# First attention of a graph-network stack on Trainium2: key projection ahead of its bank's copies, tile ends a step later, first logits amid diffusion, last two row tiles as plain products

## The chip, the cores and the metric

The kernel runs on one core of one Trainium2 chip. Its five engines are TensorE (PE, with the weight loads shown apart as PEld), VectorE (DVE), ScalarE (ACT), GpSimd (POOL) and SyncE (SP, which here issues the DMAs). The metric is the device time of one execution in microseconds; the median of several runs counts.

## The reference

A stack of four graph layers works on 3327 nodes with 256 features and a dense weighted adjacency `adj` (3327 x 3327). Each layer's output is added to its input and normalised. The change lies in layer 3, which runs two rounds of "top-p attention" and diffusion:

```python
q = X @ W1.T @ W2.T
k = X @ W3.T
probs = softmax(q @ k.T)                       # (N, N)
# per row: keep the largest probabilities until 0.9 of the mass is reached
A = probs * mask;  A = A / A.sum(-1)
...
for n in range(2):
    A = top_p_attention(Xa, W1, W2, W3)
    Xf = R @ Xf                                # R = (adj + I) / row sums: diffusion
    Xa = A @ Xa                                # attention
    Z = Z + Xf @ U1[n].T + Xa @ U2[n].T
out = layernorm(X + Z)
```

All arithmetic is in 32-bit floats.

## The kernel before, in words

The rows are cut into nt = 26 tiles of 128, and these into nh = 13 pairs (tiles 2i and 2i+1). `X` holds the features of all tiles in SBUF. The code of layers 0 to 2 and of the second round of layer 3 is the same in both kernels.

**Two products in the first round.** The first round computes, for each pair, the diffusion of its two row tiles (`diffused_pair`) and their attention (`attended_pair`). Both treat the pair as a 2 x 2 block product and do it in Strassen's manner with seven products of 128 columns each (`products`, PE) instead of eight; `b` holds the precombined blocks of `X` (in `G`'s memory), `cb` and `sw` are DVE's combinations of the other operand, and `assembled` (DVE) puts the sums in `acc` together into `c`. A diffusion pair has 13 steps; every second step issues three DMAs for an `at` buffer (three of them) and one DVE operation for `cb` (one part ahead). Tile 0's diffusion is done in layer 2's end, and tile 1's by `diffused_first`, which is a plain product of 26 blocks, 256 columns wide. An attention pair has 13 steps too; each transposes four 128 x 128 blocks of `e` with PE (`turn`) into a PSUM bank named `tp`, of which there are two, copies them to `wt` with ACT, and mixes them into `sw` with DVE three steps ahead.

**The kept rows.** `logits(t)` starts tile t: `scores` multiplies the queries with all keys in four chunks, through the one PSUM buffer `sc`, and ACT copies each chunk into `e`. POOL writes the padding columns of `e` (`L1137`). `search_short` then finds the cut: DVE takes the 8 largest of each of 26 segments (`cand`), ranks the candidates in six rounds (`top`, `rest`), ACT takes the exponential of the row (`L1382`), and DVE masks `e` in two halves. `look()` runs one step of the search at the head of the queue.

**A tile's ends.** `first` finishes a row tile in four steps: ACT scales the attention's row sums (`L1532`, into `c` itself); PE transposes the diffused row `xf` and the scaled one, and DVE copies them to `xt`; PE multiplies with `U1` and `U2` (six products), DVE adds `X` into `s`, which is sent to `sd`; PE multiplies with the second `U2` into the bank `pg`, ACT copies it to `g` (a buffer named `s`, `L1558`), which is sent to `gd`, and `key_and_query` multiplies with `wkq` into the same bank, from which ACT takes the key (`L901`) and the query (`L903`), and SP sends the query to `qd`.

**The order.** In the first round PE and DVE keep the program's order (`Fixed`, with `fixed = True`); ACT, POOL and SP are ordered by a scheduler. Most instructions of the round therefore have the helper's line, L891, and are told apart by their tiles. For each pair i the loop runs a first `stage` of seven steps (a diffusion step of pair i+1 each; the score chunks of tile 2i+2 on even steps, the ends of tile 2i-2 on odd ones; at step 5 `attend_to` finishes the search of tile 2i+1 and transposes the first blocks), then seven attention steps, then a second `stage` of six steps (scores of tile 2i+3, ends of tile 2i-1), and the other six attention steps. After the last pair the ends of tiles 24 and 25 follow one after the other.

Of the kernel before, what the change touches and what calls it, by code (L numbers as in the profile page):

```python
# [18 lines left out]
P = 128  # L19
# [31 lines left out]
def gnn_kernel(ctx: ExitStack, tc: tile.TileContext, n: int, a: dict, out: bass.AP):  # L51
# [816 lines left out]
    with tc.tile_pool(name="l3", bufs=1) as pool, tc.tile_pool(name="l3d", bufs=1, space=DRAM) as dram:  # L868
# [23 lines left out]

        tensor, vector = Fixed(nc.tensor), Fixed(nc.vector)

        def key_and_query(work, ps, p, it, xt):

            h, j = divmod(it * P, half)
            for k in range(2):
                tensor.matmul(ps, wkq[h][:, k, :], xt[:, k, :], start=(k == 0), stop=(k == 1))
            key, query = (slice(x * DA, (x + 1) * DA) for x in (h, 1 - h))  # L900
            nc.scalar.copy(kT[p][key, j:j + P], ps[key, :])  # L901
            q = work.tile([2 * DA, P], F32, name="q")
            nc.scalar.copy(q[query, :], ps[query, :])  # L903
            for x in (0, DA):
                nc.sync.dma_start(qd[p][it, x:x + DA, :], q[query, :])

        xf0 = F[:, nt - 1, :D]
        q0 = F[:, nt - 2, :P]
# [396 lines left out]
            nc.vector.scalar_tensor_tensor(d, acc, rd, t, op0=ALU.mult, op1=ALU.add)  # L1305
            out.append(d)

        def attended(work, psum, e, rhs, tp=2, copy=nc.scalar.copy):

            acc = psum.tile([P, D], F32, name="acc")  # L1310
            for j0 in range(0, nt, 4):
                m = min(4, nt - j0)
                pt = psum.tile([P, 4, P], F32, name="tp", bufs=tp)
                for j in range(m):
                    nc.tensor.transpose(pt[:, j, :], e[:, (j0 + j) * P:(j0 + j + 1) * P], ident)
                wt = work.tile([P, 4, P], F32, name="wt", bufs=3)
                copy(wt[:, :m, :], pt[:, :m, :])
                for j in range(m):
                    nc.tensor.matmul(acc, wt[:, j, :], rhs[:, j0 + j, :],  # L1319
                                     start=(j0 + j == 0), stop=(j0 + j == nt - 1))  # L1320
                yield None
            yield acc
# [199 lines left out]
        def normalizer(sm, kept, total):  # L1522

            f = t1(sm, "f")
            vector.scalar_tensor_tensor(f, total, 1e-12, kept, op0=ALU.mult, op1=ALU.max)
            vector.reciprocal(f, f)
            return f

        def first(work, psum, it, acc, f, xf, tag="pj"):

            xa = acc if tag == "tp" else work.tile([P, D], F32, name="h")
            nc.scalar.mul(xa, acc, f)  # L1532
            yield
            pt = psum.tile([P, 4, P], F32, name=tag)
            for i, v in enumerate((xf, xa)):
                for k in range(2):
                    tensor.transpose(pt[:, 2 * i + k, :], v[:, k * P:(k + 1) * P], ident)
            xt = work.tile([P, 4, P], F32, name="xt", bufs=1)
            vector.tensor_copy(xt, pt)
            yield  # L1540
            ps = psum.tile([P, 4, P], F32, name=tag).rearrange("p (k x) d -> p k (x d)", k=2)
            for k in range(4):
                tensor.matmul(ps[:, 0, :], xt[:, k, :], (u1 if k < 2 else u2)[:, 0, k % 2, :], start=(k == 0), stop=(k == 3))
            for k in range(2):
                tensor.matmul(ps[:, 1, :], xt[:, k, :], u1[:, 1, k, :], start=(k == 0), stop=(k == 1))
            s = work.tile([P, D], F32, name="s")
            vector.tensor_add(s, ps[:, 0, :], X[:, it, :])
            nc.sync.dma_start(sd[it], s)
            nc.scalar.copy(Y[:, it, :], ps[:, 1, :])
            yield  # L1550
            pg = psum.tile([P, 4, P], F32, name=tag).rearrange("p (k x) d -> p k (x d)", k=2)
            for k in range(2):
                tensor.matmul(pg[:, 0, :], xt[:, 2 + k, :], u2[:, 1, k, :], start=(k == 0), stop=(k == 1))
            if tag == "pj":
                nc.scalar.copy(G[:, it, :], pg[:, 0, :])
            else:
                g = work.tile([P, D], F32, name="s")
                nc.scalar.copy(g, pg[:, 0, :])  # L1558
                nc.sync.dma_start(gd[it], g)
            key_and_query(work, pg[:, 1, :P], 1, it, xt[:, 2:, :])  # L1560
            yield

        def second(work, psum, it, acc, f, xf):
# [48 lines left out]
        def both(*parts):  # L1612

            parts = list(parts)
            while parts:
                parts = [x for x in parts if next(x, parts) is not parts]

        with tc.tile_pool(name="l3w", bufs=2) as work, tc.tile_pool(name="l3s", bufs=4) as sm:
# [13 lines left out]
            with tc.tile_pool(name="l3p", bufs=2, space=PSUM) as psum, tc.tile_pool(name="l3a", bufs=1) as quads:  # L1632
                fixed = True
                es, searches, xfs, todo, queue = {}, {}, [xf0], [], []
                flat = G.rearrange("p t d -> p (t d)")
                b = blocks(X, [flat[:, k * nh * HD:(k + 1) * nh * HD].rearrange("p (t d) -> p t d", t=nh) for k in range(4)])

                def look():
                    while queue and next(queue[0], queue) is queue:
                        queue.pop(0)  # L1640

                def finish():
                    while queue:
                        look()

                def logits(t):
                    return start(0, t, es, searches, search_short) if t < nt else iter(())

                def spreading(i):
                    x = diffused_pair(quads, psum, i, b, xfs) if i < nh else iter(())  # L1650
                    next(x, None)
                    return x

                def stage(spread, steps, groups, ends, then=lambda: None):
                    for k in range(steps):
                        next(spread, None)
                        if k % 2:
                            next(ends, None)
                        else:
                            next(groups, None)  # L1660
                        if k == 5:
                            then()
                        look()
                    for _ in groups:
                        pass
                    for _ in ends:
                        pass

                def attend_to(i):
                    turned[0] = attended_pair(quads, psum, (es[2 * i], es[2 * i + 1]), b)  # L1670
                    finish()
                    next(turned[0])

                turned = [None]
                for _ in logits(0):
                    pass
                queue.append(searches[0])
                for _ in diffused_first(quads, psum, 1, xfs):
                    look()
                spread = spreading(1)  # L1680
                for _ in logits(1):
                    look()
                finish()
                queue.append(searches[1])
                for _ in range(8):
                    look()
                for i in range(nh):
                    ends = todo or [iter(()), iter(())]
                    stage(spread, 7, logits(2 * i + 2), ends[0], lambda: attend_to(i))
                    values = turned[0]  # L1690
                    if i + 1 < nh:
                        queue.append(searches[2 * i + 2])
                    for _ in range(7):
                        next(values)
                        look()
                    stage(spread, 6, logits(2 * i + 3), ends[1])
                    for _ in spread:
                        pass
                    finish()
                    if i + 1 < nh:  # L1700
                        queue.append(searches[2 * i + 3])
                    for k in range(6):
                        if k == 3:
                            spread = spreading(i + 2)
                        next(values)
                        look()
                        if k % 3 == 2:
                            look()
                    c = next(values)
                    todo = []  # L1710
                    for r in range(2):
                        it = 2 * i + r
                        f = normalizer(sm, kepts[0][:, it:it + 1], tots[0][:, it:it + 1])
                        todo.append(first(quads, psum, it, c[:, r, :], f, xfs[it], "tp"))
                        next(todo[r])
                for x in todo:
                    both(x)
                fl0 = unresolved(sm, psum, 0)
                fixed = False
            for x in (slice(0, JH), slice(JH, nt)):  # L1720
# [209 lines left out]
```

## Time and profile before

| what | value |
|---|---|
| median of 3 runs | 3494.32 us (3488.72 to 3496.67) |
| the profiled execution | 3488.59 us; its span 3486.7 us; mean granted PE clock 0.965 |
| busy share of the span | PE 90%, PEld 74%, DVE 79%, ACT 50%, POOL 27% |
| first attention's first scores / second attention's first scores (PE) | 1696.3 us / 2624.1 us |
| one pair of the middle | 68.46 us (the same instruction at 2059.89 and 2539.10, seven pairs apart) |

The shares are means over the whole span. For a change inside one stage the tables of waits and the timeline of that stage say more: a line of the timeline has the start, the duration, the engine, the tile written and the tiles read, the count of merged instructions, and in brackets the engine's idle time before it and what ended it. A time in the table of waits belongs to the engine that stood still; the engine after the arrow is the one whose result came last.

### The profile page before, as it was taken

To read this page: it belongs to the slowest core of one execution; us is meant where nothing else is said; L and a number is where in the kernel's file an instruction comes from. 1 tells how busy PE (TensorE), PEld (TensorE's weight loads), DVE (VectorE), ACT (ScalarE), POOL (GpSimd) and SP (SyncE) were. 2 spreads that over 40 slices of the span, in tenths; PEclk is the share of its full clock that TensorE was granted. 3 is DMA by queue.
4 is the path that set the end of the run, shared out by engine and by line. 5 is a ranking of instruction groups with operands and counts; after the bars stand their busy time and mean duration, and the time that the engine had idled before them with its cause. 6 is when DMAs were issued, how large, how long until landed. Compare 5 with 4: busy or idle time off the path is not lost. (4 is left out here: it accounts for less than half of the span.)

```text
span 3486.7 us, 50559 instructions
## 1 busy us (share of the span) xinstructions
PE 3154.8 (90%) x18379; PEld 2568.2 (74%) x18379; DVE 2759.1 (79%) x6406; ACT 1742.3 (50%) x2763; POOL 939.7 (27%) x942
## 2 busy tenths in 40 slices
PE   8999888888987777999899999999978999999996
PEld 5998767666665555888688888888865777777775
DVE  4665368999999997777577777787755999999996
ACT  1000556767767773111233333333326888888883
POOL 0000245666666652111400000000002333333332
PEclk9999999999999988999899999999998999999998
DMA  5775334334333222444222222222213122222220
GB/s 196 256 250 180 116 95 124 109 105 120 109 105 87 68 56 99 152 143 149 94 71 71 79 76 69 82 69 84 63 34 108 56 63 71 62 66 69 63 66 16
DMA packets 206264, 344.31 MB, mean 99 GB/s; under 512 B 22222, under 2 KB 129166, under 8 KB 205870
## 3 DMA queue, kind: packets, MB, share of 16 engines
q1 hardware_dynamic: 205998, 340.92, 32.1%
q8 instruction: 148, 2.42, 0.3%
q14 instruction: 118, 0.97, 0.1%
HBM read 304.65 MB, written 36.21 MB: 98 GB/s over the span
## 5 line engine op out<-in xcount | busy, mean ns | idle before, releaser
L330 POOL TENSOR_TENSOR h<-du,row 128x2048 f32<-128x2048 f32 (+1 forms) x110 | 465.8, 4235 | 344.3 <-DVE hc L330 247.2
L330 DVE TENSOR_TENSOR_SCAN h<-dA,carry,h 128x512 f32<-128x512 f32 (+1 forms) x384 | 449.1, 1221 | 18.5 <-ACT dA L337 18.4
L337 ACT ACTIVATE dA<-t,A_log 128x512 f32<-128x512 f32 (+1 forms) x448 | 293.3, 660 | 147.8 <-DVE h L330 146.3
L1286 PE MATMUL acc<-F,at 128*128 128x256 f32 x1352 | 352.1, 386 | 0.0
L1319 PE MATMUL acc<-G,wt 128*128 128x256 f32 x1352 | 335.0, 391 | 6.0 <-ACT wt L1130 5.5
L1070 PE MATMUL acc<-F,at 128*128 128x257 f32 x1352 | 302.1, 380 | 0.9 <-ACT r L1014 0.9
L389 PE MATMUL cb<-F,at 128*128 128x256 f32 x1196 | 295.0, 395 | 8.2 <-ACT hn L409 3.4
L1319 PEld LDWEIGHTS acc<-G,wt 128*128 128x128 f32 x1352 | 249.1, 192 | 65.2 <-ACT wt L1130 35.6
L1286 PEld LDWEIGHTS acc<-F,at 128*128 128x128 f32 x1352 | 238.5, 190 | 72.2 <-issue 47.8
L680 PE MATMUL y<-ident,hc 128*128 128x128 f32 x1664 | 238.5, 298 | 46.8 <-DVE hc L330 46.5
L1070 PEld LDWEIGHTS acc<-F,at 128*128 128x128 f32 x1352 | 252.4, 190 | 36.2 <-issue 1.1
L680 PEld LDWEIGHTS y<-ident,hc 128*128 128x128 f32 x1664 | 212.4, 155 | 87.0 <-DVE hc L330 62.8
L389 PEld LDWEIGHTS cb<-F,at 128*128 128x128 f32 x1196 | 229.7, 198 | 58.3 <-issue 19.9
L1137 POOL MEMSET e<- 128x1 f32 x52 | 4.9, 99 | 930.8 <-PE tp L891 807.1
L330 DVE TENSOR_TENSOR hc<-h,row 128x2048 f32<-128x2048 f32 (+2 forms) x114 | 243.8, 2140 | 11.3 <-PE y L680 4.3
L891 PEld LDWEIGHTS acc<-X,at 128*128 128x128 f32 x988 | 143.5, 194 | 49.0 <-issue 44.8
L891 PE MATMUL acc<-X,at 128*128 128x128 f32 (+1 forms) x988 | 177.9, 292 | 0.0
L891 PE MATMUL acc<-G,sw 128*128 128x128 f32 x1014 | 169.7, 276 | 6.0 <-DVE sw L891 6.0
L138 PE MATMUL acc<-t,cb 128*128 128x128 f32 (+1 forms) x1014 | 168.4, 275 | 0.0
L1253 ACT COPY wt<-tp 128x512 f32<-128x512 f32 x169 | 98.7, 588 | 131.8 <-PE tp L891 117.0
L891 PEld LDWEIGHTS acc<-G,sw 128*128 128x128 f32 x1014 | 140.3, 192 | 8.2 <-DVE sw L891 8.1
L891 DVE MAX8 cand<-e 128x8 f32<-128x128 f32 x676 | 140.8, 278 | 0.0
(412 smaller groups left out, 7095.1 us busy)
## 6 DMA issues: line engine op xcount, KB each, us to landing
at<-in_adjT SPq DMA_DIRECT2D x54, 832.0 KB, 4.4
at<-in_adjT SPq DMA_DIRECT2D x130, 320.0 KB, 3.0
row<-bc SPq DMA_DIRECT2D x80, 512.0 KB, 5.0
at<-in_adjT SPq DMA_DIRECT2D x52, 640.0 KB, 5.3
at<-in_adjT SPq DMA_DIRECT2D x52, 576.0 KB, 3.8
at<-in_adjT SPq DMA_DIRECT2D x72, 256.0 KB, 3.1
at<-mixed SPq DMA_DIRECT2D x72, 256.0 KB, 3.6
mixed<-cb SPq DMA_DIRECT2D x26, 640.0 KB, 3.9
```

What stands on the lines that cost most here:

```text
L138: mm = nc.tensor.matmul(acc, w[:, j, :], x, start=(y == 0 and k % 3 == 0 and k < 6), stop=(y == nh - 1 and k in (2, 6)))
L330: return lambda *x, **k: tc.keep_in_program_order(op(*x, **k))
L337: decays.append(op(*x, **k))
L389: ten.matmul(acc, at[:, j % JC, :], X0[:, j, :], start=(j == 0), stop=(j == nt - 1))
L680: x = ten.matmul(y[:, g * P:(g + 1) * P], h[:, g, i * P:(i + 1) * P], ident, is_transpose=True, start=(first and g == 0), stop=(last and g ...
L891: return lambda *x, **k: tc.keep_in_program_order(op(*x, **k))
L1070: nc.tensor.matmul(acc, at[:, j, :], F[:, j0 + j, :], start=(j0 + j == 0), stop=(j0 + j == nt - 1))
L1137: nc.gpsimd.memset(e[:, n:], NEG)
L1253: nc.scalar.copy(wts[-1], pt)
L1286: nc.tensor.matmul(acc, at[:, j, :], rhs[:, j0 + j, :], start=(j0 + j == 0), stop=(j0 + j == nt - 1))
L1319: nc.tensor.matmul(acc, wt[:, j, :], rhs[:, j0 + j, :], start=(j0 + j == 0), stop=(j0 + j == nt - 1))
```

## The change

There are five edits, all in the first round.

1. `key_and_query` is split. In `first`, the product with `wkq` now stands right behind the product with `U2` into the same bank, ahead of ACT's copy to `g`; the copies of key and query follow that copy.
2. In `stage`, the ends run at steps 2, 3 and 4 instead of 1, 3 and 5.
3. The score chunks of tile 1 are put between the four groups of `diffused_first`, with three `look()` after each group, where they followed it with one; pair 1's first `at` part is requested ahead of it. Seven instead of eight `look()` follow.
4. The loop over pairs runs to nh - 1, that is to pair 11. Tiles 24 and 25 are then done one by one by `attended`: 26 blocks, each a transposition and one product of 256 columns with `X`, in seven groups of four, the transpositions one group ahead and with four `wt` buffers. The ends of tiles 22 and 23, and then of 24, run between the groups; two `look()` per group of tile 24 finish the search of tile 25.
5. `first` takes the tile that it scales into as an argument.

```diff
+        def project_keys(ps, it, xt):
+            h = it * P // half
             for k in range(2):
                 tensor.matmul(ps, wkq[h][:, k, :], xt[:, k, :], start=(k == 0), stop=(k == 1))
+        def store_keys(work, ps, p, it):
...
-        def attended(work, psum, e, rhs, tp=2, copy=nc.scalar.copy):
+        def attended(work, psum, e, rhs, tp=2, copy=nc.scalar.copy, acc=None):
...
+            def turn(j0):
                 m = min(4, nt - j0)
                 pt = psum.tile([P, 4, P], F32, name="tp", bufs=tp)
                 for j in range(m):
+                    tensor.transpose(pt[:, j, :], e[:, (j0 + j) * P:(j0 + j + 1) * P], ident)
+                wts.append(work.tile([P, 4, P], F32, name="wt", bufs=4 if fixed else 3))
+                copy(wts[-1][:, :m, :], pt[:, :m, :])
+            if fixed:
+                turn(0)
+                yield None
+            for j0 in range(0, nt, 4):
+                if not fixed:
+                    turn(j0)
+                elif j0 + 4 < nt:
+                    turn(j0 + 4)
+                wt = wts.pop(0)
+                for j in range(min(4, nt - j0)):
+                    tensor.matmul(acc, wt[:, j, :], rhs[:, j0 + j, :],
...
-            key_and_query(work, pg[:, 1, :P], 1, it, xt[:, 2:, :])
+            project_keys(pg[:, 1, :P], it, xt[:, 2:, :])
+            g = G[:, it, :] if tag == "pj" else work.tile([P, D], F32, name="s")
+            nc.scalar.copy(g, pg[:, 0, :])
+            if tag != "pj":
                 nc.sync.dma_start(gd[it], g)
+            store_keys(work, pg[:, 1, :P], 1, it)
...
                     for k in range(steps):
                         next(spread, None)
-                        if k % 2:
+                        if k % 2 == 0:
+                            next(groups, None)
+                        if k in (2, 3, 4):
                             next(ends, None)
-                        else:
-                            next(groups, None)
...
+                spread = spreading(1)
+                groups = logits(1)
                 for _ in diffused_first(quads, psum, 1, xfs):
-                    look()
-                spread = spreading(1)
-                for _ in logits(1):
-                    look()
+                    next(groups, None)
+                    for _ in range(3):
+                        look()
+                for _ in groups:
+                    pass
                 finish()
                 queue.append(searches[1])
-                for _ in range(8):
+                for _ in range(7):
                     look()
-                for i in range(nh):
+                for i in range(nh - 1):
...
-                for x in todo:
-                    both(x)
+                values = attended(quads, psum, es[nt - 2], X, acc=psum.tile([P, 2, 512], F32, name="acc")[:, 0, :D])
+                next(values)
+                ends = (x for y in todo for x in y)
+                for it in (nt - 2, nt - 1):
+                    for _ in range(7):
+                        acc = next(values)
+                        if it == nt - 2:
+                            look()
+                            look()
+                        next(ends, None)
+                    acc = next(values)
+                    if it == nt - 2:
+                        finish()
+                        values = attended(quads, psum, es[nt - 1], X, acc=psum.tile([P, 2, 512], F32, name="acc")[:, 0, :D])
+                        next(values)
+                    f = normalizer(sm, kepts[0][:, it:it + 1], tots[0][:, it:it + 1])
...
+                    for _ in ends:
+                        pass
+                    ends = first(quads, psum, it, acc, f, xfs[it], "tp", c)
+                    next(ends)
+                both(ends)
```

## The prediction

> **What bounds the kernel now.** I read the table by stage first: the first attention of layer 3 runs from 1706 to 2624 us, and its middle repeats every 68.46 us (one pair of row tiles). The waits of the tensor engine in it, longest first (columns: total us, times, longest), name what the diff is about:
>
> ```profile
> PE tp L891 <- ACT c L1532: 24.5, 13, 5.6
> PE tp L891 <- ACT s L1558: 17.3, 26, 1.9
> PE acc L891 <- DVE sw L891: 8.1, 24, 1.3
> ...
> PE acc L891 <- DVE cb L891: 3.7, 1, 3.7
> ```
>
> PE stands for the scaled rows `c` and for the copy into `s`. Counted on the weight loads, so with the drained pipeline, one pair loses 1.67 us to `c` and 2 x 0.86 us to `s`. But what PE waits for is only worth its length if nothing else is as late. So next the table by windows for one pair (columns: window, length, then busy us of PE, PEld, DVE, ACT, POOL):
>
> ```profile
> 2057.96:2083.44 25.48, 22.94 (x179) 19.71 (x177) 23.02 (x84) 9.35 (x15) 0.20 (x2) 1.00 0.26 75
> 2083.44:2100.90 17.46, 16.80 (x121) 14.17 (x120) 11.70 (x33) 5.90 (x13) 0.00 (x0) 1.00 0.34 100
> 2100.90:2126.42 25.52, 25.52 (x203) 23.05 (x202) 17.15 (x60) 9.16 (x12) 0.00 (x0) 1.00 0.19 56
> ```
>
> The first window begins at the last diffusion product of a pair (I call it L) and ends at the first product with `U1` of the next (U). Its DVE share is the highest of the three, and the timeline of DVE there has one idle interval over a tenth of a us, at its start, then none until 2082.35:
>
> ```profile
> 2058.27 0.29 DVE L891 COPY c<-acc 128x128 f32<-128x128 f32 x1 [0.31 <-PE acc L891]
> ...
> 2078.66 0.69 DVE L891 TENSOR_TENSOR cb<-at 128x512 f32<-128x512 f32 x1
> ...
> 2079.05 0.44 PE L891 MATMUL tp<-ident,c 128*128 128x128 f32 x2 [1.44 <-ACT c L1532]
> ...
> 2079.78 0.39 PE L891 MATMUL acc<-G,cb 128*128 128x128 f32 x2
> ...
> 2080.03 0.68 DVE L891 COPY xt<-tp 128x512 f32<-128x512 f32 x1
> ...
> 2083.55 2.75 PE L891 MATMUL tp<-U,xt 128*128 128x256 f32 x12
> ```
>
> So from L to U the vector queue decides: it starts on the sums of L and runs through. From U to the next L, PE decides. That the wait for `c` ends at 2079.05 and the `cb` of the very next diffusion step at 2079.35 is the line to remember. Third, the tail: from 2551.51 to 2624.12 PE works 50.97 of 72.61 us, with a hole of 5.65 us and a cold clock:
>
> ```profile
> 2557.65 0.69 PE L891 MATMUL tp<-ident,c 128*128 128x128 f32 x2 [5.65 <-ACT c L1532]
> ...
> 2559.12 3.36 PE L891 MATMUL tp<-U,xt 128*128 128x256 f32 x7 [0.78 <-DVE xt L891]
> ...
> 2569.33 0.76 PE L891 MATMUL tp<-ident,e 128*128 128x128 f32 x5 [1.42 <-DVE e L891]
> ```
>
> **What the Trainium skill says.** "PSUM — Partial Sum Buffer", section on bank collisions: two engines may not touch one bank in the same quadrants at once, and the software must order them. This is the 0.86 us: `wkq`'s product goes into the bank from which ACT is copying `s`; the trace agrees. "TensorE: Matmul & The Clock Gate", section "Architectural detail": ACT and DVE queues are strictly first in, first out. The trace agrees: `cb` at 2078.66 starts as `f` ends. Same page, "What's actually happening": after an idle window of about 3.4 us the array runs at half rate until it has been busy as long. Here 8 weight loads of the `U` product take 3.06 us at 2559.12, against 12 in 2.46 us at 2083.44.
>
> **The unit prices**, from the timeline at full clock: a diffusion step 1.56 us (2073.01 to 2074.57), a score chunk 0.90, four transposes 0.44, an attention step with them 2.00, a 256-wide instruction 0.22 (two a product). One tile's ends: 0.44 (transposes), 2.68 (six `U` products), 0.90 + 0.45 (`pg`, `wkq`), 4.5 together.
>
> **Part 1, the loop (11 pairs have ends).** Removed: the waits for `s` (2 x 0.86) and for `c` (1.67), 3.4 us a pair if nothing came in their place. I follow the two queues instead.
>
> L to U: DVE runs the same list up to the `cb` of step k=0, ending 21.4 us after L (2079.35 - 2057.96). PE now does step k=2 before the transposes, and the third product of that step needs this `cb`. PE gets there about 2077.4 and waits 1.9 us: the wait for `c` becomes one for `cb`. Then 1.12 (rest of the step) + 0.90 + 0.44 + 1.56 (k=3) = 4.02, so U stands 25.46 after L, against 25.48: nothing gained. The copy `xt` now sits behind two rank rounds (0.82 each) and the second `cb`; it ends about 24.9 after L, 0.5 before it is needed.
>
> U to L: the first tile's `pg` and `wkq` lose 0.86 of wait; PE reaches the transposes of `e` 8.16 after U instead of 8.85 (2092.29 - 2083.44). The second masked half of `e` is ready at 8.44, and only the fourth transpose needs it, at 8.5: 0 to 0.25 us of new wait, I take 0.1. The 0.44 for `q` gives way to about as long for the third bank's `wt`: 0 to -0.1. The second tile's `pg` and `wkq` (1.35 us) stood after L, under DVE's list, and now stand before L, because ends come at k=4 and the last diffusion step at k=5: +1.35 on the path. Its 0.86 of wait stood after L too and was hidden, so nothing comes back for it. Sum: -0.69 + 0.1 - 0.05 + 1.35 - 0.02 = **+0.7 us a pair, +7.5 in all**. Both ends: -2 a pair, if DVE makes up the time (its slack of 0.3 at L says it doesn't), +2 if `xt` is late as well.
>
> The DMAs of the ends move with them. `sd` needs `s` after U, and lands about 1.8 us later (2564.67 to 2566.45); `g` may be written 3.8 us after U's end, so it stays hidden, with SP's three loads of `at` (1.7 us) between.
>
> **Part 2, the tail.** The loop ends one pair sooner, and tiles 24 and 25 are plain. PE's work goes up: 26 x 2 x 0.22 + 26 x 0.11 = 14.4 us a tile, 28.8 against 13 x 2.00 = 26.0. But tile 24 needs no kept rows of tile 25, so its products fill the hole while DVE masks tile 25, and the ends of 22 to 24 stand between groups. From 2551.5 on: 28.8 + 4 x 4.5 = 46.8 of work; waits: `c` of tile 22 about 2.8 (one group covers 2.7 of the hole), the first `wt` of tile 25 behind `q` and `c` on ACT 1.0, banks 1.2, cold clock 2.0; last chain: scaling 0.8, `xt` 1.2, and `s`, its DMA, `g`, `kT`, `q` past the last product 2.3. Sum 58.1, against 72.6: **-14.5**, ends -8 and -20. Earlier `wkq` spares 0.7 us of this at the very end (ACT copies follow each other where PE stood between). After it the order on all five queues is as before, so nothing else moves. Passing the scaled tile as an argument issues no instruction.
>
> **Part 3, the head.** Scores of tile 1 go between groups of `diffused_first`; before, PE took from 1719.7 to 1732.3 for them. But ACT has the exponential of tile 0 ahead of their first copy, and that needs the last segment of tile 0, whose padding POOL writes at 1714.75, after 23 scalings `F`. So copy 1 ends near 1720, PE stops after the second group, and diffusion pairs start near 1729, 3.3 us sooner. DVE's `F` of tile 1 now waits for the last group (about 1728), then the halves (3.9), 26 maxima (5.1) and two rounds: `cb` at 1740.3 instead of 1741.8. **-1.5**, ends -5 and +1. Loading pair 1 ahead puts 640 KB and three issues (1.8 us of SP) before the groups' loads; PE starts at 1706.4, so it costs 0 to 1.
>
> **Sum:** +7.5 - 14.5 - 1.5 = -8.5 us on the profiled 3488.6 us, so 3480. That execution is the fastest of those shown, 5.7 under the median of 3494.3, so against the median about **3485**. A measurement of this kernel can tell about 0.2% (7 us).
>
> **Rivals.** *The waits simply go* (PE is the bound throughout): 11 x 3.4 = 37, tail 17, head 3: -57, 3437. PE's 90% and the waits table speak for it, DVE's unbroken run from L to U against it. *Loop and tail cancel*: a tail of -10 and a loop of +8: 3491. *Slower, by DVE's chain*: `xt` behind `cb` and two rounds misses its 0.5 us of slack. If it is late by 1.8, U slips 1.3, and with 0.7 the pair costs 2 us: 22 - 10 (tail at its short end) - 1.5 = +10.5, 3505. It decides from 1.7 us a pair on at that tail, 2.1 at mine. The gap-free DVE list speaks for it; that the rounds ahead of `xt` are the same ones that already ran, against it.
>
> **Chances:** my forecast 0.52, the waits go 0.12, cancel 0.26, slower 0.10. So faster 0.64, same 0.26, slower 0.10. The forecast alone spans 3475 to 3493; the range goes on to 3460, for a part of the waits going, and to 3498.
>
> **What would show it.** Right: no PE wait for `c` in the loop but one of about 1.9 us for `cb` a pair; DVE's wait for `acc` at `c` up from 0.3 to about 1.6; a period near 69.2 us; second attention's first scores 58 us after the last paired product. Wrong: a period under 67, or PE idle from 2551.5's place to the second attention for more than 16 us.

## The result, and the profile after

The change made the kernel a little faster: 3479.06 us median (3474.8 to 3481.12) against 3494.32, ratio 0.9956 with a 95% interval of 0.9941 to 0.9971. The forecast said 3485, 3460 to 3498, with faster as the likeliest case. Measured anew at the end of the study, the ratio was 0.9973 (0.9961 to 0.9985), or 9.4 us less (5 to 14) at a kernel before of some 3490 us; the profiled executions differ by 9.5 us (3488.59 and 3479.06). The two intervals overlap (10 to 21 us and 5 to 14), and the traces speak for the lower one: the first attention, from its first scores to those of the second, is 9.7 us shorter in one trace of the changed kernel and 9.0 in the other. So the change is worth about 9 to 10 us.

The waits of PE in the first attention, after (columns as before: total us, times, longest):

```profile
PE acc L891 <- DVE cb L891: 23.6, 12, 6.2
PE acc L891 <- DVE sw L891: 18.5, 36, 1.3
...
PE tp L891 <- ACT wt L1262: 2.9, 12, 0.2
PE tp L891 <- ACT c L1553: 2.5, 1, 2.5
PE sc L1154 <- ACT q L907: 1.9, 1, 1.9
```

Read against the same table of before: 24.5 us of waits for `c` shrank to one, in the tail; the 17.3 us for `s` are gone. In their place stand 23.6 us for `cb` (3.7 before) and 18.5 for `sw` (8.1 before). Head and tail are in these sums: 6.2 of the 23.6 is one wait in the head, where the 3.7 stood. In the loop alone (1750 to 2550 us), 15.8 us for `c` and 10.2 for `s` went, and 17.4 for `cb` and 9.5 more for `sw` came: there the waits changed their names and kept their length. One pair by windows after (length, then busy us of PE, PEld, DVE, ACT, POOL; granted clock, DMA share, GB/s), cut at L, at U and between, as before:

```profile
2063.09:2088.66 25.57, 22.19 (x171) 18.89 (x169) 23.18 (x84) 8.48 (x12) 0.20 (x2) 1.00 0.22 65
2088.66:2106.15 17.49, 17.25 (x129) 15.16 (x128) 12.29 (x35) 5.96 (x14) 0.00 (x0) 1.00 0.33 99
2106.15:2132.12 25.97, 25.97 (x204) 23.40 (x202) 16.44 (x58) 9.73 (x15) 0.00 (x0) 1.00 0.23 66
```

From L to U it still takes 25.5 us, with PE busy less of it (22.19 us for 22.94) and DVE as much as before (23.18 for 23.02): PE waits for a list that is as long as it was. From U to the next L, the two other windows, it is 43.46 us for 42.98, and there PE has hardly an idle moment. The timeline of DVE and PE there, with the waits in brackets:

```profile
2063.39 0.29 DVE L891 COPY c<-acc 128x128 f32<-128x128 f32 x1 [1.63 <-PE acc L891]
...
2076.48 0.49 PE L891 MATMUL acc<-G,sw 128*128 128x128 f32 x2 [1.26 <-DVE sw L891]
...
2083.75 0.69 DVE L891 TENSOR_TENSOR cb<-at 128x512 f32<-128x512 f32 x1
2084.50 0.49 PE L891 MATMUL acc<-G,cb 128*128 128x128 f32 x2 [1.54 <-DVE cb L891]
...
2087.41 0.69 DVE L891 COPY xt<-tp 128x512 f32<-128x512 f32 x1 [0.72 <-PE tp L891]
2088.77 2.75 PE L891 MATMUL tp<-U,xt 128*128 128x256 f32 x12
```

DVE now waits 1.63 us for the sums of L, where it waited 0.31: L itself is late. Then it runs 20.4 us without a stop to `cb` at 2083.75, PE stands for that `cb`, and `xt` is ready 0.7 us ahead of U. That is the picture the forecast had drawn. The tail after:

```profile
2562.14 1.99 PE L891 MATMUL acc<-X,wt 128*128 128x256 f32 x8 [0.28 <-ACT wt L1328]
...
2566.85 0.69 PE L891 MATMUL tp<-ident,c 128*128 128x128 f32 x2 [2.49 <-ACT c L1553]
...
2609.31 3.72 PE L891 MATMUL tp<-U,xt 128*128 128x256 f32 x16 [0.78 <-DVE xt L891]
...
2615.55 0.97 PE L1154 MATMUL sc<-kT,q 64*128 64x416 f32 x4 [1.93 <-ACT q L907]
```

The hole of 5.65 us in front of `c` is 2.49 us. The last paired product, that of pair 11, ends at 2560.8, and the second attention's first scores stand 54.7 us behind it. In the kernel before, in which one more pair follows, they stand 72.6 us behind the same product.

### The profile page after: what moved, and what is told of

Same layout as the page of the kernel before. It is cut to its first block, busy times and chain, and to the rows that moved or that the text cites. A ratio compares the mean times of both kernels' runs of the same rounds, so it can differ in the third digit from the quotient of the medians.

```text
span 3477.3 us, 50356 instructions
## 1 busy us (share of the span) xinstructions
PE 3155.6 (91%) x18301; PEld 2570.0 (74%) x18301; DVE 2743.7 (79%) x6359; ACT 1738.5 (50%) x2764; POOL 938.9 (27%) x942
## 5 line engine op out<-in xcount | busy, mean ns | idle before, releaser
L891 PE MATMUL acc<-G,sw 128*128 128x128 f32 x936 | 157.2, 277 | 14.5 <-DVE sw L891 14.5
L1262 ACT COPY wt<-tp 128x512 f32<-128x512 f32 x156 | 90.4, 587 | 132.8 <-PE tp L891 116.6
L891 PE MATMUL acc<-G,cb 128*128 128x128 f32 x624 | 122.6, 278 | 23.6 <-DVE cb L891 23.6
L1403 ACT ACTIVATE e<-e,neg 128x3328 f32<-128x3328 f32 x26 | 79.8, 3070 | 127.6 <-DVE neg L891 119.6
```

Source lines behind the costliest of these rows:

```text
L891: return lambda *x, **k: tc.keep_in_program_order(op(*x, **k))
```

## The experiments

All runs are compared with the kernel before on the same chip; "us" below is the ratio times 3490. To see where a pair's time lies I cut it, in every trace, at the start of DVE's first copy of L's sums (called L here), at the six `U` products of the first tile (U), and at those of the second (U2). The pairs from the third on agree within 0.15 us, those of cb_twice apart; "both of these" is mask_early_keys_late:

| kernel | L to U | U to U2 | U2 to L | pair | ratio (95% interval) | us |
|---|---|---|---|---|---|---|
| before | 25.28 | 36.24 | 7.01 | 68.53 | | |
| keys_only | 25.28 | 35.77 | 7.01 | 68.06 | 0.9964 (0.9951-0.9978) | -12.6 |
| ends_only | 25.39 | 36.06 | 9.05 | 70.50 | 1.0077 (1.0059-1.0094) | +26.9 |
| tail_only | 25.27 | 36.24 | 7.01 | 68.51 | 0.9956 (0.9944-0.9969) | -15.4 |
| head_only | 25.27 | 36.24 | 7.01 | 68.52 | 1.0008 (1.0002-1.0015) | +2.8 |
| after | 25.39 | 35.33 | 8.33 | 69.05 | 0.9973 (0.9961-0.9985), second measurement | -9.4 |
| cb_twice | 26.13 to 27.7 | 35.33 | 8.32 | 69.78, 71.37 | 1.0035 (1.0021-1.0049) | +12.2 |
| keys_late | 25.39 | 35.33 | 7.01 | 67.73 | 0.9929 (0.9915-0.9942) | -24.8 |
| mask_early | 23.32 | 35.33 | 8.68 | 67.34 | 0.9908 (0.9893-0.9923) | -32.1 |
| both of these | 23.32 | 35.33 | 8.69 | 67.34 | 0.9917 (0.9903-0.9931) | -29.0 |
| look_early | 23.32 | 35.33 | 7.97 | 66.62 | 0.9878 (0.9860-0.9897) | -42.6 |
| look_early_old_head | 23.32 | 35.33 | 7.96 | 66.62 | 0.9888 (0.9868-0.9908) | -39.1 |
| look_twice | 23.33 | 35.33 | 7.07 | 65.73 | 0.9863 (0.9843-0.9882) | -47.8 |

**1. The parts one by one.** Each stands alone on the kernel before.

The tail (edits 4 and 5):

```diff
-                for i in range(nh):
+                for i in range(nh - 1):
...
-                for x in todo:
-                    both(x)
+                values = attended(quads, psum, es[nt - 2], X, acc=psum.tile([P, 2, 512], F32, name="acc")[:, 0, :D])
...
```

> Kernel before with the plain tail alone (rows 24 and 25 as plain products, ends spread among their groups); key projection, ends' steps and head as before. Theory (the loop's edits cost 0.6 us a pair, all of the gain is the tail's): 17 to 18 us under the kernel before, so faster than the whole change by 5 to 8 us, and a loop period of 68.5 us. Rival (the loop's edits also bring something, and the periods of the two traces differ by chance): gains 5 to 12 us, slower than the whole change.

Measured 15.4 us less (11 to 19.5), period 68.51. Its median of 3471.0 is 8 us under that of the whole change (3479); the intervals of the ratios overlap a little. From the last paired product to the second attention it takes 56.2 us here, 16.4 less than before.

The ends' steps:

```diff
-                        if k % 2:
-                            next(ends, None)
-                        else:
-                            next(groups, None)
+                        if k % 2 == 0:
+                            next(groups, None)
+                        if k in (2, 3, 4):
+                            next(ends, None)
```

> Kernel before with the ends' steps alone (k = 2, 3, 4 in place of 1, 3, 5; score groups at 0, 2, 4 as before). Theory (the vector queue decides from L to U; the second tile's g and key products move from its cover, after L, to before L): g and key products 1.35 us plus their bank wait of 0.86 us come onto the path, the wait for c becomes one for cb: plus 1.8 to 2.2 us a pair, so plus 20 to 24 us, period 70.3 to 70.7. Rival (the tensor engine is the bound and its wait for c of 1.67 us is real): minus 1 to 1.67 us a pair, minus 11 to 18 us, period 67 to 67.5.

Measured 26.9 us more (21 to 33), over the 20 to 24 that were expected; the first attention of its trace is 20.5 us longer. The period is 70.50, in the forecast 70.3 to 70.7. Its waits of PE (1750 to 2550 us) tell the two theories apart:

```profile
PE acc L891 <- DVE sw L891: 17.5, 33, 1.3
PE acc L891 <- DVE cb L891: 17.0, 11, 1.5
PE tp L891 <- ACT s L1576: 9.8, 21, 0.6
```

No wait for `c` is left, and the pair is 2 us longer all the same: the wait for `c` was a place where PE stood while DVE worked, and now it stands at `cb` and `sw`. U2 to L grew by 2.04 us, the 1.35 of `pg` and `wkq` and the better part of their bank wait, now without cover; L to U, out of which they were taken, did not shrink.

The key projection ahead of the copies:

```diff
+            project_keys(pg[:, 1, :P], it, xt[:, 2:, :])
...
             nc.scalar.copy(g, pg[:, 0, :])
...
-            key_and_query(work, pg[:, 1, :P], 1, it, xt[:, 2:, :])
+            store_keys(work, pg[:, 1, :P], 1, it)
```

> Kernel before with the key projection ahead of its bank's copies alone. Theory: the first tile's bank wait of 0.86 us lies between U and L, where the tensor engine decides, and goes (minus 0.7 to 0.86 us a pair); the second tile's lies between L and U under the vector queue and brings nothing: minus 8 to 9.5 us in all, period 67.6 to 67.8. Rival (tensor engine bound throughout): both waits go, minus 1.7 us a pair, minus 19 us, period 66.8. Second rival (the queue behind it absorbs it, a wait for the transposed e takes its place): within 2 us of the kernel before.

Measured 12.6 us less (8 to 17), period 68.06: 0.47 a pair, less than the 0.7 to 0.86 of the theory. The second tile's wait, under DVE's list, brought nothing, as said. The first tile's brought half, and the waits of PE show where most of the rest is:

```profile
PE acc L891 <- DVE sw L891: 16.0, 25, 1.3
PE tp L891 <- ACT c L1553: 15.7, 11, 1.4
PE tp L891 <- ACT q L907: 5.6, 11, 0.6
```

The wait for `q` grew from 2.2 us in 11 pairs (tail_only, which has the loop of before) to 5.6. ACT's three copies of that bank used to begin under PE's wait; now they follow each other behind `wkq`, and the transposes of `e` wait for the last. The line of `sw` (16.0 us, 8.1 in tail_only) shows where the second tile's wait went. The 0.47 us of the pairs make some 5 of the 12.6 us. Most of the rest lies in the tail, which the expectation left out: there PE waited 7.2 us for four copies into `s` in the kernel before and for none here, and from the loop's last U to the second attention it takes 124.7 us for 129.8.

The head:

```diff
+                spread = spreading(1)
+                groups = logits(1)
                 for _ in diffused_first(quads, psum, 1, xfs):
-                    look()
+                    next(groups, None)
+                    for _ in range(3):
+                        look()
...
```

> Kernel before with the head alone (first scores of tile 1 between the groups of the first diffusion, pair 1's loads ahead). Theory (the vector queue's first maxima and roundings decide when the first pair's cb comes; the traces show cb 0.5 us sooner against their own starts): 0 to 1.5 us less. Rival (the score groups' 12 us are taken off the path): minus 3 us or more. Second rival (loads of 640 KB ahead of the groups' own cost more than is gained): plus 1 us.

Measured 2.8 us more (0.7 to 5.2), so the gain that was expected is not there. The first product with `cb` for which PE waits, beside that of tail_only, which has the old head:

```profile
1743.59 0.80 PE L891 MATMUL acc<-G,cb 128*128 128x128 f32 x2 [6.21 <-DVE cb L891]
```

```profile
1741.08 0.49 PE L891 MATMUL acc<-G,cb 128*128 128x128 f32 x2 [2.33 <-DVE cb L891]
```

Counted from each trace's own first scores, this product comes at 44.95 us in head_only and at 45.02 and 45.75 in the two traces of the changed kernel; with the old head at 45.25 in tail_only and between 44.04 and 45.51 in before, keys_only and ends_only. It comes no sooner: the scores went off PE's path, and what PE waits for is DVE's chain.

**2. Is DVE's list what decides from L to U?** Doubled first, then shortened; no product moves in either.

```diff
+                for _ in range(2 if j0 == JQ else 1):
-                vector.tensor_tensor(cb[:, :, :m, :], at[:, 3:4, :m, :].to_broadcast([P, 2, m, P]), at[:, :3:2, :m, :], op=ALU.subtract)
+                    vector.tensor_tensor(cb[:, :, :m, :], at[:, 3:4, :m, :].to_broadcast([P, 2, m, P]), at[:, :3:2, :m, :], op=ALU.subtract)
```

> Changed kernel, with the cb of step k = 0 computed twice by the vector queue (0.67 us more in its list between L and U, nothing else). Theory (the queue decides there): one for one, period 69.7, plus 7 to 8 us against the changed kernel. Rival (the queue is only as busy as it has to be, the tensor engine decides): no difference within 2 us.

```diff
+                    finish()
                     for _ in spread:
                         pass
-                    finish()
```

> Changed kernel, with the last masked half of e (1.95 us of the vector queue) issued ahead of the pair's assembly c instead of behind it; no product of the tensor engine moves. Theory (the vector queue's list from L to U decides): it fills the 1.63 us in which the queue waits for the sums of L, and the list gets 1.6 us shorter: L to U 23.8 instead of 25.39, period 67.4 instead of 69.04, 17 to 18 us under the changed kernel, 33 under the kernel before. Rival (the tensor engine is the bound, or the wait for cb is set by a transfer): the same time as the changed kernel within 4 us. Second rival (the sums' copy, 0.3 us later, makes something else late): up to 3 us slower than the changed kernel.

One `cb` more (0.67 us) made L to U longer by 0.74 us (26.13), about one for one. But most pairs, eight of eleven, took 2.3 us more, and the run lost some 22 us against the changed kernel (+12.2 for -9.4) instead of 8. The table by windows shows the same work in two neighbouring pairs:

```profile
1991.83:2063.20 71.37, 67.02 (x498) 58.55 (x497) 52.70 (x178) 24.19 (x39) 0.20 (x2) 0.98 0.25 72
2063.20:2132.98 69.78, 65.43 (x498) 57.46 (x497) 52.73 (x178) 24.18 (x39) 0.20 (x2) 1.00 0.26 74
```

DVE is equally busy; PE is busy 1.6 us longer at a mean granted clock of 0.98 (the third number from the end). PE's wait for `cb` is 2.27 us here, and in the first of these two pairs the granted clock behind it, from 2023.5 to 2027.8, is 0.53 and then 0.66.

Taking the last masked half (1.95 us) out of the list brought 22.7 us against the changed kernel (-32.1 for -9.4): 1.7 us a pair, and more in two places where the mask has no part in it. The first pair's period fell from 71.01 to 67.70, by 1.6 us beyond the rest: PE waits for `cb` there as long as in the changed kernel (1.91 us, 1.90 there), but the granted clock stays at 1.00 behind it; the last section shows when it falls. In the tail the clock stays up too, and it takes 53.1 us for 54.7. L to U is 23.32. The order of PE is untouched, so PE as the bound is excluded there, and so is a transfer behind `cb`, since none was moved. L came 0.35 us later (8.68), since the masks now end after its sums.

**3. The second tile's products back behind L.**

```diff
-                def stage(spread, steps, groups, ends, then=lambda: None):
+                def stage(spread, steps, groups, ends, then=lambda: None, at=(2, 3, 4)):
...
-                        if k in (2, 3, 4):
+                        if k in at:
...
-                    stage(spread, 6, logits(2 * i + 3), ends[1])
+                    stage(spread, 6, logits(2 * i + 3), ends[1], at=(2, 3, 5))
```

> Changed kernel, with the second tile's g and key products at k = 5 (behind L) instead of k = 4; the first tile's ends stay at 2, 3, 4. Theory: 1.35 us go back under the vector queue's list: U to L 7.0 instead of 8.33, L to U 25.3 to 25.5 as before, period 67.7, 15 us under the changed kernel. Rival (tensor engine the bound): same products, period 69.0, the same time.

Period 67.73, forecast 67.7; U2 to L is 7.01 again, and L to U does not change although it holds 1.35 us more of PE. These 1.32 us a pair are the forecast's term of 1.35, shown alone. The run is 15.4 us under the changed kernel; the clock kept up in its first pair too (68.09 us).

With this and the mask ahead of the assembly, both edits above:

> Changed kernel with both: last masked half ahead of the assembly, second tile's g and key products behind L. Theory: from L to U the queue needs 23.8 us and the tensor engine, with 1.35 more, some 24.0 to 24.7, so the two meet: period 66.3 to 67.0, 22 to 30 us under the changed kernel. Rival (each of the two only shifts the same wait): period 67.4, no better than the better of them alone.

The rival was right: a period of 67.34, exactly mask_early alone. The run stands 3.1 us behind mask_early; the intervals overlap, and 1.6 of it is the first pair, 69.31 us for 67.70, in which the clock fell again. With L's sums ready earlier, DVE was not: from the second tile's `s` on it runs through crossing, masks and assembly. The last two kernels pull the search forward, into the 4 us in which DVE waits for the transposes of the second tile:

```diff
                         look()
+                        if steps == 6 and k == 1:
+                            look()
```

> As the kernel with the mask ahead of the assembly and the second tile's g and key products behind L, and one more step of the search issued at k = 1 of the second stage, where the vector queue is idle for 4 us, so that both masked halves come one diffusion step sooner. Theory (in that kernel the vector queue ran through from the second tile's s to U, so what bounded it was the start of the masks after U, not their place behind L): U to L back to 7.0 from 8.69 with L to U still at 23.3, period 65.7 to 65.9, 17 us under that kernel, 3440 to 3445 us at a kernel before of 3490. Rival (the tensor engine's own work from L to U, with its 0.86 and 1.3 us waits, does not fit in 23.3): period 66.5 to 67.3. Second rival (the earlier look delays xt or s, so U slips): no gain.

Period 66.62, short of the 65.8 and in the rival's range, but not for the rival's reason: L to U is 23.32 still, and it is U2 to L that came down to 7.97 only. The timeline of DVE shows what I had miscounted:

```profile
2050.68 0.42 DVE L891 TENSOR_TENSOR s<-tp,X 128x256 f32<-128x256 f32 x1 [2.85 <-PE tp L891]
2051.03 0.15 DVE L891 TENSOR_SCALAR lim<-tot 128x1 f32<-128x1 f32 x1
...
2051.91 1.95 DVE L891 SCALAR_TENSOR_TENSOR e<-e,v 128x1664 f32<-128x1664 f32 x1
...
2055.86 0.29 DVE L891 COPY c<-acc 128x128 f32<-128x128 f32 x1
```

The step moved ahead of `s` was the last rank round, not the crossing; the crossing still stood behind `s`, and no idle time is left before the copy at 2055.86. So a second step:

```diff
-                        if steps == 6 and k == 1:
+                        if steps == 6 and k < 2:
```

> As look_early, with a second extra step of the search, at k = 0 of the second stage, so that the crossing stands ahead of the second tile's s and the first masked half right behind it. In look_early crossing and masks still followed s, 5.2 us in a row, and ended 0.95 us after the sums of L. Theory: with the crossing (0.9 us) ahead of s the masks end about when L's sums do: U to L 7.0 to 7.2, period 65.7 to 65.9, 8 to 10 us under look_early. Rival (the crossing waits for the scalar engine's exponential of the top values and so holds up s, or xt): period 66.6 or more.

Period 65.73, as forecast. The mask begins as `s` ends, and the copy of L's sums is 7.07 us behind U2:

```profile
2041.32 0.42 DVE L891 TENSOR_TENSOR s<-tp,X 128x256 f32<-128x256 f32 x1 [2.36 <-PE tp L891]
2041.66 1.94 DVE L891 SCALAR_TENSOR_TENSOR e<-e,v 128x1664 f32<-128x1664 f32 x1
...
2045.60 0.28 DVE L891 COPY c<-acc 128x128 f32<-128x128 f32 x1
```

This version beats both kernels: 3441.5 us, ratio 0.9863 to the kernel before. PE is busy 64.05 of the 65.73 us of a pair; the rest is mostly its wait for `cb`, 1.5 us.

Last, look_early with the head of before:

```diff
...
-                    next(groups, None)
-                    for _ in range(3):
-                        look()
+                    look()
...
```

> The same with the head of the kernel before (first scores of tile 1 after the first diffusion, pair 1's loads after it). Theory (the head's edit gains nothing: its longer wait for cb, 6.2 us against 2.3 to 3.7, leaves the tensor engine's clock cold behind it): 1 to 4 us faster than with the new head. Rival (the new head is worth the 0.5 to 1.5 us of the forecast): 0.5 to 1.5 us slower.

Inconclusive: 0.9888 (0.9868 to 0.9908) with the old head, 0.9878 (0.9860 to 0.9897) with the new, so neither of the two expectations can be told from the other.

**4. The size of the whole.**

> The changed kernel itself, measured anew. Theory (the parts in the traces, a tail of minus 17.9, a loop of plus 8.3, a head of about nothing, make the whole of it): minus 8 to minus 12 us against the kernel before, whose median was 3489.3 to 3489.6 in each of the later comparisons. Rival (the difference of 15.3 us between the first medians holds, and about 5 us of it lie outside these parts): minus 14 to minus 17 us.

0.9973, or -9.4 us (-13.6 to -5.2), as the parts in the traces make it. No run has all the edits but the second.

## Why the prediction was right, and where it was off

**The bound.** Right. L to U was said to stay (25.46 for 25.48) because DVE's list decides; it stayed in before, keys_only, ends_only and after within 0.11 us, whatever PE had to do in it. It moved about one for one when DVE's list did: +0.74 for 0.67 us more, -2.07 for 1.95 less.

**The wait that takes the place.** Right: none for `c` in the loop, one for `cb` of 1.54 us a pair (said: 1.9), DVE's wait for the sums at `c` 1.63 (said: 1.6). What the forecast did not name is the second substitute: with `pg`, `wkq` and their bank wait gone from behind L, PE reaches the products with `sw` too early and waits there 1.5 us a pair, where it was 0.7 (18.5 and 8.1 us in 12 pairs).

**The loop's sum.** Said +0.7 a pair, +7.5; the pair grew by 0.52 (69.05 for 68.53; the 68.46 of the forecast is a mean over seven pairs, the last four of them 0.13 shorter). The large term, +1.35 for `pg` and `wkq` before L, measured 1.32. The terms of -0.69, +0.1 and -0.05 for the first tile measured -0.91 (U to U2, 36.24 to 35.33), where the forecast took 0.69 for a wait that it had put at 0.86 and did not say why; keys_only has -0.47 of it and ends_only -0.18, and the rest appears only with both edits. From the first pair's `U` products to the last paired product it is 750.2 us for 741.9, so +8.3: 2.0 of that is one pair that the forecast did not have, the first, with 71.01 in both profiled executions. There PE waits 1.90 us for `cb`, 0.36 longer than later, and then runs at half the clock for one stretch, which costs the other 1.6. So the +8.3 lies near the +7.5 by luck: a pair cost less than said, and the fall of the clock, which nothing in the forecast stood for, made up for it.

**The parts don't add.** ends_only costs 2.0 a pair and keys_only saves 0.47, and together they cost 0.52, not 1.5: moved ahead of L alone, the ends bring the bank wait of 0.86 with them, and the key projection takes it away there. Edit 1 was worth more beside edit 2 than alone, and edit 2 was a loss both alone (2.0) and beside edit 1 (0.99, 69.05 for 68.06).

**The tail.** Said 58.1 us, measured 54.7: -17.9 instead of -14.5. The work was sized rightly (46.8 said; 48.7 busy, of which some 1.6 by the clock of 0.97 over the stretch). The mis-sized terms: 1.2 for bank waits, of which none is left, since edit 1 takes them out here too (tail_only, without it, has 0.46, 0.51, 0.51 and 1.62 and needs 56.2); 1.0 for the first `wt` of tile 25, measured 0.24; 4.3 for the last chain, measured 0.35 + 0.78 + 1.93 = 3.1.

**The head.** Said -1.5, not seen. The term that failed is "about 1728" for the end of the last group: DVE's `F` came at 1730.49, 1.4 us later than said when the trace's own start, 1.1 us later than before, is taken off; 0.8 of that is the first group's later start, which was named as a possible cost. With the halves, the maxima and two rounds as sized, `cb` came at 1741.69, and that is 0.5 us sooner than before by the same count: less than the old head's own spread over four traces. Why the head lost 2.8 us alone (0.7 to 5.2) stays open; its wait for `cb` is longer (6.2 us for 2.3 to 3.7), and beside look_early nothing can be told.

**The sum** of the traces is +8.3 - 17.9 - 0.1 = -9.7 in the first attention (918.1 us for 927.8 from its first scores to those of the second), against -8.5 forecast: the tail 3.4 us better than said, the loop 0.8 and the head 1.4 worse. That the sum is off by only 1.2 us is in part luck, as these misses cancel. "The waits simply go" is excluded by ends_only, "slower by DVE's chain" did not come since `xt` kept its slack; "loop and tail cancel" had the loop right, and the tail too short.

## What to carry to other kernels

A wait in the table of waits is worth its length only if nothing else ends just behind it: look for the stretch in which another engine's queue runs without a gap, and count the change against that queue. Under such a queue, work of the waiting engine is free (keys_late put 1.35 us of it back there, and L to U stayed at 25.39), so moving it out to where that engine decides costs its full length, here 1.32 us a pair. What helps is to shorten the queue itself, by moving its own work into its idle time elsewhere: here three such moves, with the second tile's products put back, brought 38 us more, where the change had brought 9. What the putting back has of it beside the last two moves, no run shows.

## What the hardware showed that I had not expected

The clock fell after shorter waits than I had counted with. The Trainium skill, "TensorE: Matmul & The Clock Gate", section "What's actually happening", gives an idle window of about 3.4 us, free-running, after which the array runs at half rate. The traces agree on the window: in each of the fourteen, all changes of the granted clock lie on one grid of 3.413 us, within 0.01 us over the whole span. They do not agree that it must be idle. Between 1698 and 2620 us, taken over all the traces, 68 windows of the grid at full clock were followed by one at half the clock. PE did nothing in 14 of them and was busy in the other 54, for up to 0.49 of the window; in all the windows that were followed by the full clock it was busy for 0.46 or more. So it is not the length of a wait alone that decides, but how much of it falls into one window. The wait of 1.90 us in the first pair, in the changed kernel and then in keys_late:

```profile
1873.87:1877.28 3.41, 1.52 (x12) 1.40 (x14) 2.91 (x14) 0.91 (x2) 0.00 (x0) 1.00 0.63 176
1877.28:1880.69 3.41, 3.41 (x14) 2.23 (x13) 1.60 (x4) 0.85 (x1) 0.00 (x0) 0.50 0.08 23
```

```profile
1872.84:1876.25 3.41, 2.49 (x20) 2.08 (x18) 3.04 (x15) 2.68 (x4) 0.00 (x0) 1.00 0.03 5
1876.25:1879.66 3.41, 2.43 (x16) 1.71 (x17) 2.83 (x8) 0.73 (x3) 0.00 (x0) 1.00 0.64 188
1879.66:1883.07 3.41, 3.41 (x26) 3.23 (x25) 0.98 (x2) 1.08 (x2) 0.00 (x0) 1.00 0.08 11
```

In the changed kernel the wait, from 1873.86 to 1875.76, lies in one window and leaves PE 1.52 us of work; in keys_late, from 1875.33 to 1877.23, it is shared by two, which keep 2.49 and 2.43. So the same wait brought the clock down in both traces of the changed kernel and in mask_early_keys_late, and not in keys_late, mask_early and look_early. The waits of 1.54 us, which leave over half of a window wherever they fall, never did it; those of 2.27 in cb_twice did in eight pairs of eleven, at a price of 1.6 us each. And one of 3.48 us in the tail of mask_early_keys_late, shared by two windows that were busy for 0.52 and 0.47, did not.

The first scores of layer 3 began between 1691.0 and 1706.5 us in the profiled executions, though all instructions before them are the same. That spread is larger than the change; only the pieces within one trace showed its parts.
